# Second biases at eviction or in the residual, router columns beside an identity, expert rows turned amid the tile ahead

## The chip, the cores and the metric

The kernel runs on one core of one Trainium2 chip. The metric is the device time of one execution in microseconds (us). TensorE (PE) multiplies matrices, VectorE (DVE), ScalarE (ACT) and GpSimd (POOL) work elementwise, and SyncE (SP) issues most DMA transfers. Each engine takes its instructions in the order in which the program lists them for it, and waits on semaphores for the others.

## The reference

Two layers of attention and feed-forward parts run over x of shape (16, 256, 256) in float32. The change lies in the last line, the mixture of experts:

```python
h = gelu(x @ fc1_w.T + fc1_b)                      # conditioned part, exact gelu
y = concat([h @ fc2_w.T + fc2_b, h @ We.T + be])   # 192 shared columns, 64 of the sequence's own expert
probs = softmax(y @ w_router.T)                    # 8 experts
gates = the two largest probs, else 0
acc = gelu(y @ Ws1.T + bs1) @ Ws2.T + bs2          # shared expert, tanh gelu
acc = acc + sum over e of gates[e] * (gelu(y @ W1[e].T + b1[e]) @ W2[e].T + b2[e])
x = x + acc / sqrt(1 + 2 / 8)
```

There are 4096 tokens (16 sequences of 256), model width 256, hidden width 1024. The factor 1 / sqrt(1.25) is `OUT_SCALE`.

## The kernel before, in words

`woven(k)` computes everything ahead of the mixture, in an order planned by `weave`, and writes x to memory. It is not touched. `mixture` (from line 1034) then works on tiles of 128 tokens, four to a block, eight blocks. Its instructions are ordered by the framework: each engine's list follows a planned schedule in which ready instructions of a later block may go ahead of an earlier one's. PSUM banks come from two rings of four, `bank0` and `bank1`, chosen by `k.stream`; a ring gives out a bank again when its readers are done.

- `conditioned` (L1340), once per block: eight transposes of x (`transposed`, L99; copies alternate between ACT and DVE, L113), fc1 with exact gelu, the shared and own columns of fc2 into `yT` (features on partitions), router logits with a matmul of 8 columns (L1401), then `route`.
- `route` (L1202): softmax and the two best experts on DVE, with a short exp on ACT. `r.g` takes the gates (L1225), with a ninth column of ones. Small bf16 matmuls count how many tokens went to each expert before. Then y is turned back to tokens on partitions (L1255) and copied into one of three buffers `r_y` (L1257). GpSimd scatters the rows by indirect DMA into `ysort`, sorted by expert (L1259), two scatters per tile of 128 tokens.
- `plan_tiles` (L1267) works out which expert each tile of 256 sorted rows belongs to.
- `shared_block` (L1087): the shared expert on a block. The gates are transposed to `gT` (L1093, L1094). After the eight matmuls of the second layer a ninth, `gT` against `k.b2` (L1108), adds the sum over experts of gate times b2, and bs2 by the column of ones. DVE adds the scaled bank to x (L1111). Four blocks run before the experts, four after.
- `expert_tile` (L1114): 39 at most, 35 of them always, the last four within a branch that isn't taken with these inputs. Per tile: index and b1 are copied to `own_b1`, SP reads expert and row from it, loads `ys` (256 rows), `w1` and `w2`; four transposes turn `ys` to `ysT`; 16 matmuls with gelu (L1140), 16 more, a copy to `o` (L1145), a store to `osort`. Two buffers each. In the built order the transposes of two tiles stand together ahead of the first of them.
- `combine` (L1149): GpSimd gathers a token's two expert rows from `osort`, DVE adds them by their gates to x, SP stores.

Of the kernel before, what the change touches and what calls it, by code (L numbers as in the profile page):

```python
# [19 lines left out]
P = 128  # L20
S = 256
D = 256
# [1011 lines left out]
def mixture(k, out):  # L1034

    nc, tc, a = k.nc, k.tc, k.a
    B, NT = k.B, 2 * k.B
    with ExitStack() as ctx:  # L1040
        k.ps = ctx.enter_context(tc.tile_pool(name="ps", bufs=4, space=bass.MemoryType.PSUM))
        keep = ctx.enter_context(tc.tile_pool(name="moe_keep", bufs=1))

        k.xs = keep.tile([P, NT, D], F32, name="xs")
        for b in range(B):
            nc.sync.dma_start(out=k.xs[:, 2 * b : 2 * b + 2, :], in_=k.xd[b].rearrange("(s p) d -> p s d", p=P))
        k.hp = ctx.enter_context(tc.tile_pool(name="moe_h", bufs=2))
        k.p2 = ctx.enter_context(tc.tile_pool(name="moe_p2", bufs=2))
        k.yT = keep.tile([P, 2, B * S], F32, name="yT")
        k.b1 = keep.tile([P, NE + 1, 8], F32, name="b1")  # L1050
        k.b2 = keep.tile([NE + 1, D], F32, name="b2")
        nc.sync.dma_start(out=k.b1, in_=a["b1"])
        nc.sync.dma_start(out=k.b2, in_=a["b2"])
        r = routing_state(k, keep)
        w1s = keep.tile([P, 2, FF1], F32, name="w1s")
        w2s = keep.tile([P, 8, D], F32, name="w2s")
        nc.sync.dma_start(out=w1s, in_=a["w1"][NE])
        nc.sync.dma_start(out=w2s, in_=a["w2"][NE])
        conditioned(k, keep, r)
        k.stream = 1  # L1060
        plan_tiles(k, keep, r)

        ew = ctx.enter_context(tc.tile_pool(name="moe_w", bufs=2))
        early = 4
        for blk in range(early):
            k.stream = blk % 2
            shared_block(k, r, w1s, w2s, blk)
        for t in range(k.n_tiles - SPARE):
            k.stream = t % 2
            expert_tile(k, ew, r, t)  # L1070

        used = nc.values_load(r.used[0:1, 0:1], min_val=0, max_val=k.n_tiles)
        with tc.If(used > k.n_tiles - SPARE):
            for t in range(k.n_tiles - SPARE, k.n_tiles):
                k.stream = t % 2
                expert_tile(k, ew, r, t)
        for blk in range(early, NT // 4):

            for t in range(4 * (blk - early), 4 * (blk - early) + 4):
                combine(k, r, t, out)  # L1080
            k.stream = blk % 2
            shared_block(k, r, w1s, w2s, blk)
            for t in range(4 * blk, 4 * blk + 4):
                combine(k, r, t, out)


def shared_block(k, r, w1, w2, blk):  # L1087

    nc = k.nc
    gT = k.p2.tile([NE + 1, 512], F32, name="gT", tag="gT")  # L1090
    pt = bank(k)
    for i in range(4):
        nc.tensor.transpose(pt[: NE + 1, i * P : (i + 1) * P], r.g[:, 4 * blk + i, :], k.ident)  # L1093
    nc.vector.tensor_copy(gT, pt[: NE + 1, :])  # L1094
    hT = k.hp.tile([P, 8, 512], F32, name="hT", tag="hT")
    for f in range(8):
        ph = bank(k)
        mm(
            nc,
            ph,  # L1100
            [(w1[:, c, f * P : (f + 1) * P], k.yT[:, c, blk * 512 : (blk + 1) * 512]) for c in range(2)],
        )
        nc.scalar.activation(hT[:, f, :], ph, AF.Gelu_apprx_tanh, bias=k.b1[:, NE, f : f + 1])  # L1103
    for t4 in range(4):
        t = 4 * blk + t4
        po = bank(k)[:, :D]
        pairs = [(hT[:, f, t4 * P : (t4 + 1) * P], w2[:, f, :]) for f in range(8)]
        pairs.append((gT[:, t4 * P : (t4 + 1) * P], k.b2))  # L1108
        mm(nc, po, pairs)
        x = k.xs[:, t, :]  # L1110
        nc.vector.scalar_tensor_tensor(x, po, OUT_SCALE, x, ALU.mult, ALU.add)  # L1111


def expert_tile(k, pool, r, t):  # L1114

    nc, a = k.nc, k.a

# [9 lines left out]
    nc.sync.dma_start(out=ys, in_=k.ysort[bass.ds(row, TT), :].rearrange("(c p) d -> p c d", p=P))  # L1127
    nc.sync.dma_start(out=w1, in_=a["w1"][bass.ds(e, 1)].rearrange("e p c f -> p (e c) f"))
    nc.sync.dma_start(out=w2, in_=a["w2"][bass.ds(e, 1)].rearrange("e p f d -> p (e f) d"))
    ysT = k.p2.tile([P, 2, TT], F32, name="ysT", tag="ysT")  # L1130
    transposed(
        k,
        ysT.rearrange("p c (s t) -> p (c s) t", t=P),
        [ys[:, s, c * P : (c + 1) * P] for c in range(2) for s in range(2)],
    )
    hT = k.p2.tile([P, 8, TT], F32, name="ehT", tag="ehT")
    for f in range(8):
        ph = bank(k)[:, :TT]
        mm(nc, ph, [(w1[:, c, f * P : (f + 1) * P], ysT[:, c, :]) for c in range(2)])
        nc.scalar.activation(hT[:, f, :], ph, AF.Gelu_apprx_tanh, bias=b1[:, f : f + 1])  # L1140
    po = bank(k).rearrange("p (s d) -> p s d", s=2)
    for s in range(2):
        mm(nc, po[:, s, :], [(hT[:, f, s * P : (s + 1) * P], w2[:, f, :]) for f in range(8)])
    o = k.p2.tile([P, 2, D], F32, name="eo", tag="eo")
    nc.vector.tensor_copy(o, po)  # L1145
    nc.sync.dma_start(out=k.osort[t * TT : (t + 1) * TT, :].rearrange("(c p) d -> p c d", p=P), in_=o)


def combine(k, r, t, out):  # L1149
# [19 lines left out]
def routing_state(k, keep):  # L1169
    nc = k.nc  # L1170
    NT = 2 * k.B
    r = Routing()
    r.g = keep.tile([P, NT, NE + 1], F32, name="g_all")
    nc.gpsimd.memset(r.g, 1.0)
    r.hot = keep.tile([P, TOPK, NT, NE], F32, name="hot")
    r.rank = keep.tile([P, NT, NE], F32, name="rank")
    r.gate = keep.tile([P, TOPK, NT], F32, name="gate")
# [21 lines left out]
    return r  # L1199


def route(k, r, pool, logits, t0, n):  # L1202

    nc = k.nc
    B_ = lambda t: t.unsqueeze(2).to_broadcast([P, n, NE])
# [16 lines left out]
    nc.vector.tensor_tensor(gt, gt, eq, ALU.add)  # L1222
    place = pool.tile([P, n, NE], F32, name="r_place", tag="r_place")
    nc.vector.tensor_reduce(place, gt, AX.X, ALU.add)
    nc.vector.scalar_tensor_tensor(r.g[:, t0 : t0 + n, 0:NE], place, TOPK - 0.5, p, ALU.is_lt, ALU.mult)  # L1225
    tmp = pool.tile([P, n, NE], F32, name="r_tmp", tag="r_tmp")
    for i in range(TOPK):
        hot = r.hot[:, i, t0 : t0 + n, :]
# [20 lines left out]
    nc.vector.tensor_copy(posi, pos)  # L1249

    for t in range(n):
        pt = bank(k)[:, :D]
        tok = slice((t0 + t) * P, (t0 + t + 1) * P)
        for c in range(2):
            nc.tensor.transpose(pt[:, c * P : (c + 1) * P], k.yT[:, c, tok], k.ident)  # L1255
        y = pool.tile([P, D], F32, name="r_y", tag="r_y", bufs=3)
        copies(k)(y, pt)  # L1257
        for i in range(TOPK):
            nc.gpsimd.indirect_dma_start(  # L1259
                out=k.ysort[:, :],  # L1260
                out_offset=bass.IndirectOffsetOnAxis(ap=posi[:, i, t : t + 1], axis=0),
                in_=y,
                in_offset=None,
            )

# [74 lines left out]
def conditioned(k, keep, r):  # L1340
# [3 lines left out]
    with ExitStack() as ctx:  # L1344
# [9 lines left out]
        fc1b = load("fc1b", [P, 8], a["fc1b"])  # L1354
        fc2 = load("fc2", [P, 8, P], a["fc2a"])
        fc2b = load("fc2b", [P, 1], a["fc2_b"][0:P].unsqueeze(1))
        wr = load("wr", [P, 2, NE], a["w_router"])
        expb = load("expb", [16, 64], a["L1_cond2_experts_b"])

        bias2 = w.tile([P, B], F32, name="bias2")  # L1360
# [11 lines left out]
        for blk in range(NT // 4):  # L1372
            k.stream = blk % 2
            for b in (2 * blk, 2 * blk + 1):
# [18 lines left out]
            for i in range(2):  # L1393
# [1 line left out]
                py = bank(k)[:, :S]  # L1395
                mm(nc, py, [(own[b % 3][:, f, :], hT[:, f, i * S : (i + 1) * S]) for f in range(8)])
                nc.vector.tensor_scalar(k.yT[:, 1, b * S : (b + 1) * S], py, bias2[:, b : b + 1], None, ALU.add)
# [112 lines left out]
```

## Time and profile before

| | |
|---|---|
| median of 3 runs | 2944.68 us (2943.74 to 2948.99) |
| the profiled execution | 2943.53 us, its span 2941.8 us |
| mean clock granted to TensorE | 0.963 |
| TensorE busy over the span | 2768.7 us, 94% |
| DVE, ACT, POOL busy | 1428.6, 924.0, 842.2 us |
| first transposes of the mixture | 1907.59 us from the start |
| conditioned blocks | routers from 1955.29 us to 2173.97 us |
| first expert transposes | 2301.67 us |
| last four shared blocks | from 2812.74 us |

In a group's name `out<-in` the tiles are named without their numbers; a line can be that of a helper, so L49 stands for every matmul made by `mm`. An f32 matmul appears as two instructions. TensorE's instructions overlap, so differences between starts say more than lengths do. A wait is put down to the releaser that came last.

### The profile page before, as it was taken

Reading aid. Unit: us, or ns where it says so; the run is one execution under the profiler, and the core shown is the slowest. Engines: PE = TensorE matmul, PEld = TensorE weight load, DVE = VectorE, ACT = ScalarE, POOL = GpSimd, SP = SyncE. Lnnn points to the kernel's source line nnn. Section 1 sums busy time; section 2 is a strip of 40 time slices with the busy share of each in tenths; the row PEclk is TensorE's granted clock in tenths of the full one; section 3 lists DMA queues with packets and bytes.
Section 4 is the critical chain, followed back from the end, with each engine's and each line's share of the span. In section 5 each row is a group of like instructions: output and inputs, shape, how many; then the busy total and the mean of one; then the engine's idle time right before and its main releaser. Section 6 shows DMA issues by size and latency. Waiting matters only on the chain. (4 is left out here: it accounts for less than half of the span.)

```text
span 2941.8 us, 42036 instructions
## 1 busy us (share of the span) xinstructions
PE 2768.7 (94%) x15979; PEld 2072.5 (70%) x15979; DVE 1428.6 (49%) x3073; ACT 924.0 (31%) x2416; POOL 842.2 (29%) x1023
## 2 busy tenths in 40 slices
PE   5899999999999999999999989689999999999999
PEld 3666667777777777767777767545566888888865
DVE  6566666676676676675776655413240000000023
ACT  2223333333333333423334333223321222222221
POOL 4333333433344343343343333202220000000034
PEclk7799999999899999999999999889999999999999
DMA  3122122122122132222221222231111355555523
GB/s 107 55 93 73 53 92 84 56 80 74 59 91 69 58 97 69 63 92 69 64 92 35 76 90 74 87 93 51 51 38 67 108 179 179 179 181 179 177 85 95
DMA packets 191230, 265.66 MB, mean 90 GB/s; under 512 B 34217, under 2 KB 161970, under 8 KB 181682
## 3 DMA queue, kind: packets, MB, share of 16 engines
q1 hardware_dynamic: 184882, 246.16, 26.2%
q0 software_dynamic: 6144, 16.79, 1.8%
q8 instruction: 128, 2.10, 0.3%
q14 instruction: 76, 0.62, 0.1%
HBM read 202.34 MB, written 60.56 MB: 89 GB/s over the span
## 5 line engine op out<-in xcount | busy, mean ns | idle before, releaser
L160 ACT ACTIVATE f_prob<-pair,f_stat 128x144 f32<-128x144 f32 x512 | 190.7, 377 | 270.2 <-DVE f_stat L160 258.8
L160 DVE TENSOR_TENSOR pair<-pair,mask 128x256 f32<-128x256 f32 (+1 forms) x384 | 197.8, 516 | 123.1 <-PE pair L160 83.2
L49 PE MATMUL bank<-ysT,w 128*128 128x256 f32 x1120 | 249.3, 381 | 5.7 <-ACT ysT L113 5.7
L160 PE MATMUL single<-e_zT,wq 128*128 128x256 f32 x1024 | 254.1, 392 | 0.0
L1155 POOL DMA_INDIRECT got<-osort,pos_o x64 | 62.3, 973 | 662.8 <-ACT hT L1103 608.5
L49 PE MATMUL bank<-w,ehT 128*128 128x256 f32 x1120 | 247.4, 379 | 0.0
L49 PEld LDWEIGHTS bank<-ysT,w 128*128 128x128 f32 x1120 | 211.3, 190 | 38.0 <-ACT ysT L113 9.9
L49 PEld LDWEIGHTS bank<-w,ehT 128*128 128x128 f32 x1120 | 212.8, 190 | 28.9
L160 PEld LDWEIGHTS single<-e_zT,wq 128*128 128x128 f32 x1024 | 193.4, 196 | 32.9 <-issue 2.7
L1140 ACT ACTIVATE ehT<-bank,own_b 128x256 f32<-128x256 f32 x280 | 132.5, 473 | 241.6 <-PE bank L49 241.6
L160 POOL TENSOR_SCALAR_AFFINE_SELECT b_e<-b_e 128x512 f32<-128x512 f32 x128 | 86.5, 676 | 329.9 <-ACT b_e L160 329.9
L160 PE MATMUL pair<-keys,f_q 32*128 32x144 f32 x2048 | 164.9, 300 | 0.9 <-ACT b_e L160 0.7
L160 PEld LDWEIGHTS pair<-keys,f_q 32*128 32x128 f32 x2048 | 137.2, 190 | 35.9 <-issue 28.6
L160 ACT ACTIVATE b_e<-pair 128x768 f32<-128x768 f32 x128 | 103.6, 810 | 166.4 <-PE pair L160 153.3
L160 PE MATMUL single<-wo,f_oT 128*128 128x256 f32 x512 | 129.8, 386 | 9.5 <-ACT f_oT L160 8.4
L160 POOL TENSOR_TENSOR f_q<-f_t,f_t 128x256 f32<-128x256 f32 x128 | 91.6, 734 | 160.9 <-DVE f_t L160 151.4
L160 PE MATMUL pair<-b_qkT 16*128 16x128 f32 (+1 forms) x1024 | 127.3, 373 | 11.0 <-ACT b_qkT L160 8.0
L1145 DVE COPY eo<-bank 128x512 f32<-128x512 f32 x35 | 24.2, 692 | 230.9 <-PE bank L49 230.9
L160 DVE TENSOR_REDUCE qpad<-pair 128x2 f32<-128x256 f32 (+1 forms) x256 | 131.0, 554 | 4.4
L1259 POOL DMA_INDIRECT ysort<-r_y,r_posi x64 | 62.6, 978 | 241.0 <-DMA ysort<-r_y,r_posi 97.0
L160 DVE TENSOR_TENSOR x<-x,single 128x512 f32<-128x512 f32 (+1 forms) x112 | 68.0, 607 | 128.7 <-PE single L160 128.1
L160 POOL TENSOR_TENSOR keys<-f_t,f_t 128x256 f32<-128x256 f32 x128 | 95.2, 762 | 118.8 <-DVE f_t L160 117.6
(295 smaller groups left out, 5319.7 us busy)
## 6 DMA issues: line engine op xcount, KB each, us to landing
w<-in_w SPq DMA_DIRECT2D x70, 1024.0 KB
ysort<-zero SPq DMA_DIRECT2D x32, 1024.0 KB
wq<-in_w_qk SPq DMA_DIRECT2D x128, 256.0 KB
wv<-in_w_v SPq DMA_DIRECT2D x64, 256.0 KB
wo<-in_w_out SPq DMA_DIRECT2D x64, 256.0 KB
ys<-ysort SPq DMA_DIRECT2D x35, 256.0 KB
osort<-eo SPq DMA_DIRECT2D x35, 256.0 KB
xT<-in_xT SPq DMA_DIRECT2D x16, 256.0 KB
```

The source lines that it names most:

```text
L49: nc.tensor.matmul(out, lhsT, rhs, start=start and i == 0, stop=stop and i == last)
L160: return Op([(self.name, self.cost(fn, outs, aps), lambda: call(*args, **kw))], outs, aps)
L1140: nc.scalar.activation(hT[:, f, :], ph, AF.Gelu_apprx_tanh, bias=b1[:, f : f + 1])
L1145: nc.vector.tensor_copy(o, po)
L1155: nc.gpsimd.indirect_dma_start(out=g, out_offset=None, in_=k.osort[:, :], in_offset=bass.IndirectOffsetOnAxis(ap=r.pos_o[:, i, t : t + 1], ...
L1259: nc.gpsimd.indirect_dma_start(out=k.ysort[:, :], out_offset=bass.IndirectOffsetOnAxis(ap=posi[:, i, t : t + 1], axis=0), in_=y, in_offset ...
```

## The change

The second biases leave TensorE. bs2, times `OUT_SCALE`, is broadcast over the partitions, and GpSimd adds it to a block's x once that block's x has been transposed. Each expert's b2 is loaded with its weights, broadcast, and added when a tile's bank is evicted; so the gates need no transposing and `r.g` is gone.

The router's matrix gets an identity of 128 columns ahead of its 8: one matmul of 136 columns per half of the features gives the half of y turned to tokens, and that half's share of the logits. The two shares lie side by side in a bank; DVE copies one and adds the other to it. y is copied out before routing, into one of five buffers, and `route` gets it as `ys`.

`expert_tile` becomes `expert_rows` (loads and transposes) and `expert_tiles` (the rest), and the rows of tile t + 1 are asked for between the two matmul runs of tile t. In the built order tiles 0 and 1 are still turned together, and each later tile's transposes stand between the runs of the tile ahead. The order on SP keeps a tile's loads of ys, w1 and w2 ahead of the store of o two tiles before; the load of b2 stands behind that store.

```diff
-        k.b2 = keep.tile([NE + 1, D], F32, name="b2")
+        k.bs2 = keep.tile([P, D], F32, name="bs2")
         nc.sync.dma_start(out=k.b1, in_=a["b1"])
-        nc.sync.dma_start(out=k.b2, in_=a["b2"])
+        nc.sync.dma_start(out=k.bs2, in_=a["b2"][NE : NE + 1].to_broadcast([P, D]))
+        nc.vector.tensor_scalar(k.bs2, k.bs2, OUT_SCALE, None, ALU.mult)
...
-        for t in range(k.n_tiles - SPARE):
-            k.stream = t % 2
-            expert_tile(k, ew, r, t)
+        expert_tiles(k, ew, r, range(k.n_tiles - SPARE))
...
@@ def shared_block
-    gT = k.p2.tile([NE + 1, 512], F32, name="gT", tag="gT")
-    pt = bank(k)
-    for i in range(4):
-        nc.tensor.transpose(pt[: NE + 1, i * P : (i + 1) * P], r.g[:, 4 * blk + i, :], k.ident)
-    nc.vector.tensor_copy(gT, pt[: NE + 1, :])
...
-        pairs = [(hT[:, f, t4 * P : (t4 + 1) * P], w2[:, f, :]) for f in range(8)]
-        pairs.append((gT[:, t4 * P : (t4 + 1) * P], k.b2))
-        mm(nc, po, pairs)
+        mm(nc, po, [(hT[:, f, t4 * P : (t4 + 1) * P], w2[:, f, :]) for f in range(8)])
...
-def expert_tile(k, pool, r, t):
+def expert_rows(k, pool, r, t):
+    k.stream = t % 2
...
     nc.sync.dma_start(out=w2, in_=a["w2"][bass.ds(e, 1)].rearrange("e p f d -> p (e f) d"))
+    b2 = k.p2.tile([P, D], F32, name="eb2", tag="eb2")
+    nc.sync.dma_start(out=b2, in_=a["b2"][bass.ds(e, 1)].to_broadcast([P, D]))
     ysT = k.p2.tile([P, 2, TT], F32, name="ysT", tag="ysT")
     transposed(
...
+    return ysT, w1, w2, b1, b2
+
+def expert_tiles(k, pool, r, tiles):
+    nc = k.nc
+    rows = expert_rows(k, pool, r, tiles[0])
+    for t in tiles:
+        ysT, w1, w2, b1, b2 = rows
+        k.stream = t % 2
+        hT = k.p2.tile([P, 8, TT], F32, name="ehT", tag="ehT")
+        for f in range(8):
+            ph = bank(k)[:, :TT]
+            mm(nc, ph, [(w1[:, c, f * P : (f + 1) * P], ysT[:, c, :]) for c in range(2)])
+            nc.scalar.activation(hT[:, f, :], ph, AF.Gelu_apprx_tanh, bias=b1[:, f : f + 1])
+        if t + 1 in tiles:
+            rows = expert_rows(k, pool, r, t + 1)
+            k.stream = t % 2
+        po = bank(k).rearrange("p (s d) -> p s d", s=2)
+        for s in range(2):
+            mm(nc, po[:, s, :], [(hT[:, f, s * P : (s + 1) * P], w2[:, f, :]) for f in range(8)])
+        o = k.p2.tile([P, 2, D], F32, name="eo", tag="eo")
+        nc.vector.tensor_tensor(o, po, b2.unsqueeze(1).to_broadcast([P, 2, D]), ALU.add)
...
@@ def routing_state
-    r.g = keep.tile([P, NT, NE + 1], F32, name="g_all")
-    nc.gpsimd.memset(r.g, 1.0)
...
@@ def route
-    nc.vector.scalar_tensor_tensor(r.g[:, t0 : t0 + n, 0:NE], place, TOPK - 0.5, p, ALU.is_lt, ALU.mult)
...
-        pt = bank(k)[:, :D]
-        tok = slice((t0 + t) * P, (t0 + t + 1) * P)
-        for c in range(2):
-            nc.tensor.transpose(pt[:, c * P : (c + 1) * P], k.yT[:, c, tok], k.ident)
-        y = pool.tile([P, D], F32, name="r_y", tag="r_y", bufs=3)
-        copies(k)(y, pt)
...
-                in_=y,
+                in_=ys[t],
...
@@ def conditioned
-        wr = load("wr", [P, 2, NE], a["w_router"])
+        wr = w.tile([P, 2, P + NE], F32, name="wr")
+        nc.sync.dma_start(out=wr[:, :, P:], in_=a["w_router"])
+        nc.vector.tensor_copy(wr[:, :, 0:P], k.ident.unsqueeze(1).to_broadcast([P, 2, P]))
...
+            x = k.xs[:, 4 * blk : 4 * blk + 4, :]
+            nc.gpsimd.tensor_tensor(x, x, k.bs2.unsqueeze(1).to_broadcast([P, 4, D]), ALU.add)
...
-            pl = bank(k)[:, : 4 * NE].rearrange("p (t e) -> p t e", e=NE)
+            logits = p2.tile([P, 4, NE], F32, name="logits", tag="logits")
+            part = p2.tile([P, 4, NE], F32, name="part", tag="part")
+            ys = []
             for t4 in range(4):
                 tok = slice(blk * 512 + t4 * P, blk * 512 + (t4 + 1) * P)
-                mm(nc, pl[:, t4, :], [(k.yT[:, c, tok], wr[:, c, :]) for c in range(2)])
-            logits = p2.tile([P, 4, NE], F32, name="logits", tag="logits")
-            nc.vector.tensor_copy(logits, pl)
-            route(k, r, p2, logits, 4 * blk, 4)
+                py = bank(k)[:, : 2 * (P + NE)].rearrange("p (c w) -> p c w", c=2)
+                for c in range(2):
+                    mm(nc, py[:, c, :], [(k.yT[:, c, tok], wr[:, c, :])])
+                nc.vector.tensor_copy(part[:, t4, :], py[:, 1, P:])
+                nc.vector.tensor_tensor(logits[:, t4, :], py[:, 0, P:], part[:, t4, :], ALU.add)
+                y = p2.tile([P, 2, P], F32, name="r_y", tag="r_y", bufs=5)
+                copies(k)(y, py[:, :, 0:P])
+                ys.append(y.rearrange("p c d -> p (c d)"))
+            route(k, r, p2, logits, ys, 4 * blk, 4)
```

More of the change, by code (lines that the diff above doesn't have):

```diff
@@ L1067, in mixture @@
             shared_block(k, r, w1s, w2s, blk)
-        for t in range(k.n_tiles - SPARE):
-            k.stream = t % 2
-            expert_tile(k, ew, r, t)
+        expert_tiles(k, ew, r, range(k.n_tiles - SPARE))
         used = nc.values_load(r.used[0:1, 0:1], min_val=0, max_val=k.n_tiles)
         with tc.If(used > k.n_tiles - SPARE):
-            for t in range(k.n_tiles - SPARE, k.n_tiles):
-                k.stream = t % 2
-                expert_tile(k, ew, r, t)
+            expert_tiles(k, ew, r, range(k.n_tiles - SPARE, k.n_tiles))
         for blk in range(early, NT // 4):
@@ L1135, in expert_tile @@
     )
[L1136 to L1146, printed above, removed]
+    return ysT, w1, w2, b1, b2
[18 more added lines that the diff above has]
+        nc.vector.tensor_tensor(o, po, b2.unsqueeze(1).to_broadcast([P, 2, D]), ALU.add)
+        nc.sync.dma_start(out=k.osort[t * TT : (t + 1) * TT, :].rearrange("(c p) d -> p c d", p=P), in_=o)
 def combine(k, r, t, out):
@@ L1199, in routing_state, with route @@
     return r
-def route(k, r, pool, logits, t0, n):
+def route(k, r, pool, logits, ys, t0, n):
     nc = k.nc
```

## The prediction

> **What bounds the kernel now.** I read the page's slices first, then the stretches from 1926 us on, which are the mixture, and there TensorE's own waits. The page says TensorE is busy 94% of the span, but that is a mean over a woven part that this change leaves alone. Three stretches of the mixture, with the busy time of each engine:
>
> ```profile
> core 0: us, PE busy (x) PEld busy (x) DVE busy (x) ACT busy (x) POOL busy (x), PEclk, DMA share, GB/s
> 2048.45:2079.83 31.38, 31.38 (x121) 18.71 (x120) 8.96 (x37) 9.51 (x14) 7.67 (x8) 1.00 0.17 51
> ...
> 2330.73:2359.79 29.06, 28.77 (x137) 25.17 (x136) 2.56 (x7) 8.16 (x17) 0.00 (x0) 1.00 0.54 182
> 2844.51:2875.15 30.64, 30.64 (x105) 18.89 (x105) 9.46 (x21) 5.50 (x8) 15.63 (x16) 1.00 0.34 100
> ```
>
> They are one block of the conditioned stage, two expert tiles, and one shared block without its first transposes. TensorE fills each at clock 1.00 and nobody else is half busy, so here a TensorE instruction removed is time removed, until somebody is late. The waits of TensorE from 1990 to 2302 us are none; from 2302 to 2812 us there is one kind:
>
> ```profile
> PE bank L49 <- ACT ysT L113: 5.7, 18, 0.7
> ```
>
> The timeline of a shared block shows what its bias costs (start, length, line, tile, count):
>
> ```profile
> 2270.49 0.60 PE L1093 MATMUL bank<-ident,g_all 128*9 128x128 f32 x4
> 2270.93 13.90 PE L49 MATMUL bank<-yT,w1s 128*128 128x512 f32 x32
> 2284.67 3.62 PE L49 MATMUL bank<-w2s,hT 128*128 128x256 f32 x16
> 2288.22 0.69 PE L49 MATMUL bank<-b,gT 9*128 9x256 f32 x2
> 2288.84 3.72 PE L49 MATMUL bank<-w2s,hT 128*128 128x256 f32 x16
> 2292.49 0.69 PE L49 MATMUL bank<-b,gT 9*128 9x256 f32 x2
> ```
>
> Lengths overlap, so I work with distances of starts. An f32 matmul is two instructions. 32 of 512 columns take 13.74 us (2270.93 to 2284.67), 0.429 each. A token group with its bias recurs every 4.27 us (2288.22 to 2292.49).
>
> An expert pair (requests are on SP's queue):
>
> ```profile
> 2326.11 0.38 SPq L1127 DMA_DIRECT2D ys<-ysort  x1
> 2330.73 1.04 PE L107 MATMUL bank<-ident,ys 128*128 128x128 f32 x8
> 2331.42 0.58 ACT L113 COPY ysT<-bank 128x512 f32<-128x512 f32 x1 [6.92 <-PE bank L107]
> 2332.06 7.17 PE L49 MATMUL bank<-ysT,w 128*128 128x256 f32 x32 [0.29 <-ACT ysT L113]
> ```
>
> Within a pair the runs of 32 follow each other at 6.90 us (2316.92, 2323.82, 2330.73), so 0.2157 a matmul instruction. The turning plus its wait is 1.33 us (2330.73 to 2332.06), of which eight transposes are 0.92.
>
> The router of a block:
>
> ```profile
> 1985.70 1.18 PE L49 MATMUL bank<-wr,yT 128*128 128x8 f32 x10
> 1986.73 0.74 PE L107 MATMUL bank<-ident,xs 128*128 128x128 f32 x5
> 1987.31 0.73 PE L49 MATMUL bank<-wr,yT 128*128 128x8 f32 x6
> 1987.90 0.52 PE L107 MATMUL bank<-ident,xs 128*128 128x128 f32 x3
> 1988.26 6.37 PE L49 MATMUL bank<-g_xT,fc 128*128 128x512 f32 x14
> ...
> 1994.67 1.07 PE L1255 MATMUL bank<-ident,yT 128*128 128x128 f32 x8
> ```
>
> Ten matmul instructions of 8 columns take 1.03 us, 0.103 each; a transpose 0.115. The turning of y holds TensorE 0.91 us (1994.67 to the next start, 1995.58).
>
> **What the Trainium skill says.** "TensorE: Matmul & The Clock Gate", LDWEIGHTS: the load's time goes with the columns of the weights, not with the rows contracted. The trace agrees: gT's 9-row loads have a median of 182 ns, 128-row ones 190. A bias of 9 rows is priced like a full matmul. "FP8 and Floating Point Precision", TensorE Precision Notes: true FP32 takes four passes; 0.429 and 0.2157 us for 512 and 256 columns, two instructions to a matmul, fit that. "SBUF — State Buffer", Who interferes with whom: a VectorE instruction with two SBUF inputs contends with a GpSimd one that reads SBUF. In this kernel's router stage GpSimd computes nothing, so no trace of before shows it. "DMA: Bandwidth & Descriptors", Specifications: pieces under 512 B are below line rate; it bears on wr's loading.
>
> **1. Shared blocks (8).** Gone are four transposes of g_all (0.44 us), one copy on DVE, and four bias matmuls. From 2239.32 to 2270.49 a block is 31.17 us. What stays is 13.74 + 64 x 0.2157 = 13.81, together 27.55. Gain 3.62 us, which is more than the 8 bias instructions at 0.2157 (1.73) plus 0.44: the rest is the switch to 9 rows and back. 8 x 3.62 = **29.0 us**. In the last four blocks GpSimd's gathers must keep up: 16 of them 1.25 us apart are 20 us, in a block of 27.5, and two per token group (2.5 us) against a group of 3.45. Before, GpSimd still waited 6.5 us in each of those blocks, so TensorE stays the bound and the end (evict, two adds, store) moves with it. With that cover gone the price would be at most a few us at the very end.
>
> **2. Expert tiles (35).** By the built streams, TensorE turns tiles 0 and 1 together, then tile t+1 between the two matmul runs of tile t. Per pair before: 29.06. After, a tile is 6.91 + 0.46 + 6.90, and the ysT copies (0.58 on ACT, 0.69 on DVE) lie under the 6.9 us second run. Before, 2301.67 to about 2810.95 is 509.3. After: 1.33 + 0.1 first fill + 35 x 13.81 + 33 x 0.46 = 500.0. Gain **9.3 us**. Bounds: no gain if four transposes inside a tile cost an exposed 0.27 more than at its edge; not above 9.4, since only the waits go.
> What moves with it: the eviction adds b2 instead of copying; an add from PSUM of the same 128x512 is 0.69 us in the woven part, the copy 0.69, so nothing. The new 128 KB load of b2 stands on SP after the store of o, whose buffers it also waits for; about 0.4 us of SP plus its register setup, against an SP gap of over 5 us before the next request. It is needed a tile later. DMA share goes from 0.54 by a twentieth. On DVE the index copy that SP waits for now stands, for every second tile, behind the ysT copy, so requests slip about 1.4 us. ys is due at the end of the first run of the next tile: 6.9 x 2 less about 3.7, plus 0.5, is 10.5 us after its request. In the profile above the pair's second ys was asked for at 2326.11 and used from about 2331.2 with no wait, so it lands within 5.1 us.
>
> **3. Router (8 blocks).** Removed: eight transposes, 0.91. Widened: 16 instructions from 8 to 136 columns. From 0.429 and 0.2157 the slope is 0.000833 us a column, so 136 columns are 0.116 against 0.103: +0.2. Blocks 0 and 7 gain 0.7 each. Between blocks 1 to 6 and their successors the old order split the router's matmuls around xs transposes; the built stream has all 16, then all 8. The fourth transpose then ends at 1.86 + 0.46 = 2.32 us after the router's start, the ACT copy begins 0.24 later and takes 0.58, and the next matmuls start at 3.19 instead of 2.56. Against this +0.63 stand 0.91 and about 0.2 of an old wait for the second copy: gain 0.48 each.
> VectorE has six more small operations a block, and evicts y before it routes (0.42 twice on DVE, twice on ACT); r_p comes about 0.4 us later by that. GpSimd's addition of bs2, 128x1024, is 1.9 us by its f_prob multiplication of that shape in the woven part, and falls about 3 us after the router's start, just when routing uses two SBUF inputs; if it blocks them, sel comes another 1.1 us later, at about +8.9 to +9.7, and TensorE wants it at +9.3. I take 0.2 us of wait per block, bounds 0 and 0.6. Sum 1.4 + 6 x (0.48 - 0.2) = **3.1 us**, from -1 to 5.
> Behind DVE's y copy stands the second xT copy, for which TensorE waits. That copy needs one of five y buffers, freed when six scatters of the block before are done. Scatters follow each other like this:
>
> ```profile
> 2074.39 0.96 POOL L1259 DMA_INDIRECT ysort<-r_y,r_posi  x1 [1.71 <-DMA ysort<-r_y,r_posi]
> 2077.55 0.96 POOL L1259 DMA_INDIRECT ysort<-r_y,r_posi  x1 [2.20 <-DVE yT L1397]
> ```
>
> They start 12.1 us after the router (2048.45 to 2060.55); the sixth is done by +29.1. The copy falls at 30.7 + 2.6 = 33.3. Slack 4 us, or 2 to 3 if routing is late; 1 to 2 for block 0, whose scatters shared the queues with weights.
>
> **4. Start of the mixture.** TensorE waits for expb until 1923.48. Ahead of it in the queue bs2 now moves 128 KB instead of 9, 0.4 us at the about 330 GB/s of those 20 us, and wr 256 pieces of 32 B instead of 128 of 64. The new DVE copies (wr 0.4, bs2 0.4) lie in DVE's idle 19.96 us there, and GpSimd drops a memset off the path. Loss **0.6 us**, bounds 0 and 3.
>
> **Sum.** 29.0 + 9.3 + 3.1 - 0.6 = 40.8. The profiled execution took 2943.5 (span 2941.8), so 2902.7 (span 2901.0). The median of the runs is 1.2 above it: **2903.9 us**.
>
> **Rivals.**
> - The router gives its gain back: y buffers or GpSimd's addition make TensorE wait 1 to 3 us in seven blocks. For it: the thin slack of block 0. Against it: 4 us elsewhere. 2911 to 2925. Chance 0.12.
> - The expert order doesn't pay: transposes amid a tile cost 0.27 us more than at its edge. Against it: 2330.73 follows the run before without a gap. 2913. Chance 0.08.
> - Slower: ys is late for its new, earlier place. TensorE would stop in 34 tiles in front of the transposes. Every us that ys lands beyond 10.5 after its request costs 34; from 11.7 it eats all 40.8, and at 13 the time is 2989. Against it: the 5.1 us bound, at a DMA share of 0.54. Chance 0.03.
> - A little more than forecast, where bank or copy waits that I left in vanish at the start or the branch: 2890 to 2896. Chance 0.05.
> - Nothing moves, within 0.2% (6 us, about what a measurement of this kernel can tell from no change): it needs two of the losses together. Chance 0.01.
> The forecast has 0.71, its own range 2897 to 2911. The range to 2894 and 2917 takes in most of the first two rivals and part of the fourth. Faster 0.95, same 0.01, slower 0.04.
>
> **What would show it.** Shared blocks 27.5 us apart with no line of g_all or gT. Expert tiles 14.27 us apart, with TensorE's wait for ysT once. Routers 30.7 us apart, their 16 instructions in 1.9, and a wait of 0.4 for the g_xT copy. Wrong would be: TensorE waiting for ys from DMA; DVE's r_y copies waiting for DMA with g_xT behind them; TensorE waiting for r_sel over 0.5 us; a clock under 1.00 after 1960 us.

## The result, and the profile after

The changed kernel takes 2901.68 us in the median of five runs (2893.57 to 2905.76), the kernel before 2944.68 us beside it. The ratio is 0.9853, with a 95% interval of 0.9836 to 0.9870. The forecast was 2903.9 us. The profiled execution took 2904.1 us, its span 2902.4 us, 39.4 us below the span before.

The five runs span 12 us, so that the median lies 2.2 us from the forecast is partly luck; the parts show more. Where the 39.4 us lie, as distances between starts of TensorE's instructions in the two profiles:

| stretch | before | after | difference | forecast |
|---|---|---|---|---|
| start of the span to the first router | 1955.29 | 1955.85 | +0.6 | +0.6 |
| eight routers (0.7, 6 x 0.08, 0.8; worked out below) | | | -1.9 | -3.1 |
| shared blocks, each | 31.17 | 27.55 | 8 x -3.62 = -29.0 | -29.0 |
| first expert transposes to the late shared blocks | 511.07 | 501.47 | -9.6 | -9.3 |
| after the last shared block: last additions and stores | | | +0.5 | 0 |

The expert row has the pause at the branch in it, for which TensorE waits 2.0 us in the changed kernel and 1.6 in the kernel before; without the pause the gain there is 10.0 us.

The same kinds of stretches as shown for before, each with the busy time of every engine: one conditioned block, two expert tiles, one shared block:

```profile
2048.18:2079.48 31.30, 30.83 (x113) 18.19 (x112) 11.32 (x43) 9.42 (x14) 10.06 (x9) 1.00 0.17 51
2287.11:2315.62 28.51, 28.51 (x134) 25.13 (x135) 1.81 (x7) 8.17 (x17) 0.00 (x0) 1.00 0.42 143
2814.92:2842.47 27.55, 27.55 (x98) 18.24 (x96) 9.28 (x20) 5.50 (x8) 16.84 (x18) 1.00 0.44 127
```

TensorE still fills the expert and shared stretches. The first row is the only one in which it no longer does: 31.30 us long, 30.83 busy. The missing 0.47 is in the list of its waits from 1956 to 2302 us (total, times, longest). Before, this list was empty here.

```profile
PE bank L49 <- ACT g_xT L113: 2.7, 6, 0.5
PE bank L49 <- ACT ysT L113: 0.2, 1, 0.2
```

The second line stands for the experts: one wait of 0.2 where there were 18. In TensorE's timeline an expert tile's turning stands between two full runs, without a gap, every 14.25 us:

```profile
2457.80 7.07 PE L49 MATMUL bank<-ysT,w 128*128 128x256 f32 x32
2464.71 0.60 PE L107 MATMUL bank<-ident,ys 128*128 128x128 f32 x4
2465.14 7.07 PE L49 MATMUL bank<-w,ehT 128*128 128x256 f32 x32
```

A shared block is two lines in place of ten, and the next block follows at 2258.28:

```profile
2230.74 13.90 PE L49 MATMUL bank<-yT,w1s 128*128 128x512 f32 x32
2244.47 13.98 PE L49 MATMUL bank<-w2s,hT 128*128 128x256 f32 x64
```

The router of a block:

```profile
2048.18 2.02 PE L49 MATMUL bank<-wr,yT 128*128 128x136 f32 x16
2050.04 1.04 PE L107 MATMUL bank<-ident,xs 128*128 128x128 f32 x8
2051.55 6.28 PE L49 MATMUL bank<-g_xT,fc 128*128 128x512 f32 x14 [0.47 <-ACT g_xT L113]
2057.66 0.17 PE L49 MATMUL bank<-r_sel,earlier 128*128 128x8 bf16 x1
...
2057.90 3.25 PE L49 MATMUL bank<-g_xT,fc 128*128 128x512 f32 x7
```

fc1 starts 3.37 us after the router (2.57 before) and goes on after the counting matmuls (L49, r_sel and seen) at +9.72 (+9.88 before). Most of the router's story lies between these two numbers, and most of the experiments are about them.

### The profile page after: what moved, and what is told of

Its sections match the earlier page's. It is cut to its first block, busy times and chain, and to the rows that moved or that the text cites. A ratio compares the mean times of both kernels' runs of the same rounds, so it can differ in the third digit from the quotient of the medians.

```text
span 2902.4 us, 41871 instructions
## 1 busy us (share of the span) xinstructions
PE 2728.9 (94%) x15819; PEld 2056.7 (71%) x15819; DVE 1437.1 (50%) x3115; ACT 925.0 (32%) x2416; POOL 862.8 (30%) x1030
## 5 line engine op out<-in xcount | busy, mean ns | idle before, releaser
L49 PE MATMUL bank<-ysT,w 128*128 128x256 f32 x1120 | 247.5, 379 | 0.2 <-ACT ysT L113 0.2
L49 PE MATMUL bank<-w,ehT 128*128 128x256 f32 x1120 | 247.5, 379 | 0.0
L49 PEld LDWEIGHTS bank<-ysT,w 128*128 128x128 f32 x1120 | 212.7, 190 | 29.4 <-ACT ysT L113 0.5
L49 PEld LDWEIGHTS bank<-w,ehT 128*128 128x128 f32 x1120 | 210.2, 190 | 27.2
L1152 DVE TENSOR_TENSOR eo<-bank,eb 128x512 f32<-128x512 f32 x35 | 24.2, 692 | 234.4 <-PE bank L49 234.4
L160 PE MATMUL pair<-b_qS,b_qkT 17*128 17x256 f32 (+1 forms) x1024 | 121.7, 357 | 6.2 <-DVE qpad L160 2.8
```

What stands on the lines that cost most here:

```text
L49: nc.tensor.matmul(out, lhsT, rhs, start=start and i == 0, stop=stop and i == last)
L160: return Op([(self.name, self.cost(fn, outs, aps), lambda: call(*args, **kw))], outs, aps)
L1152: nc.vector.tensor_tensor(o, po, b2.unsqueeze(1).to_broadcast([P, 2, D]), ALU.add)
```

## Experiments

The woven part ahead of the mixture varies by over ten us from execution to execution: the first router starts between 1944.9 and 1959.2 us in profiles of kernels whose woven part is the same, and before's own medians beside these experiments lay between 2936.0 and 2943.3. So small effects are read in distances inside the mixture, which repeat to 0.1 us, but for the pause at the branch (0.9 to 2.0 us). For the eight conditioned blocks I use the distance from the first router to the second shared block's first matmul, less one shared block, and in the kernels with g_all less 0.43 us for its first transposes. It is 221.7 us before and 219.8 after: the router's 1.9.

### Biases alone, on the kernel before

```diff
-        k.b2 = keep.tile([NE + 1, D], F32, name="b2")
+        k.bs2 = keep.tile([P, D], F32, name="bs2")
...
-    gT = k.p2.tile([NE + 1, 512], F32, name="gT", tag="gT")
...
-        pairs.append((gT[:, t4 * P : (t4 + 1) * P], k.b2))
...
-    nc.vector.tensor_copy(o, po)
+    nc.vector.tensor_tensor(o, po, b2.unsqueeze(1).to_broadcast([P, 2, D]), ALU.add)
...
+            nc.gpsimd.tensor_tensor(x, x, k.bs2.unsqueeze(1).to_broadcast([P, 4, D]), ALU.add)
```

> The kernel before with the biases alone: bs2 added by GpSimd in the conditioned stage, b2 at the expert tiles' eviction, no g_all, no gT, no bias matmul. My theory: the shared blocks give what they gave in the whole change, 8 x 3.62 = 29.0 us, each 27.55 apart; the larger load of bs2 costs at most 0.4 at the start; the addition at the eviction costs nothing. 2944.7 - 28.6 = 2916. In the old router VectorE's r_p stands 0.2 us later than the addition's start too, so the addition delays r_sel by up to 1.8 us; if TensorE waits for that, blocks 1 to 6 of the conditioned stage are 31.4 to 33 apart instead of 31.38, and the time is 2916 to 2926. Rival: the gain belonged to the three parts together; this part alone gives less than 26.

Measured: 2917.05 us against 2943.27 of before beside it, ratio 0.9922 (0.9896 to 0.9948). Shared blocks are 27.55 apart, expert tiles as before. But the conditioned blocks grew by 5.0 us (221.7 to 226.7), blocks 3 to 6 from 31.38 to 31.96 each, blocks 1 and 2 more (33.22 and 32.15). VectorE's r_p takes 1.83 us there instead of 0.18 and ends with GpSimd's addition (2045.92 and 2045.87). So the 29.0 us are the biases' own, the rival falls, and the addition has a price, 5 us in this company; whether all of the 5 us is the addition's, the experiments with the old router and with the additions moved take up.

### Expert order alone, on the kernel before

```diff
-        for t in range(k.n_tiles - SPARE):
-            k.stream = t % 2
-            expert_tile(k, ew, r, t)
+        expert_tiles(k, ew, r, range(k.n_tiles - SPARE))
```

(with `expert_rows` and `expert_tiles` of the change, without b2)

> The kernel before with the expert order alone: tile t+1's rows are turned between the two matmul runs of tile t, b2 stays in the shared blocks. My theory: tiles 14.25 to 14.27 apart instead of 14.53 a tile, one wait for ysT instead of 18, so 9.3 to 9.6 us less: 2935.1. Rival: part of the 9.6 came from the eviction or from b2's load; then less than 9 here and the rest in the biases alone. The conditioned stage and the shared blocks stay as before (31.38 and 31.17 apart).

Measured: 2934.0 us against 2943.27, ratio 0.9976 (0.9964 to 0.9988). From the first expert transposes to the first late matmul 501.61 us instead of 511.50, so 9.9 us less; conditioned and shared blocks to 0.01 as before. The order's gain is its own. The whole change has 9.6 and not 9.9 because its pause at the branch is 0.4 longer, so b2's load and addition at the eviction cost nothing that shows.

### The changed kernel with the old router

```diff
-        wr = w.tile([P, 2, P + NE], F32, name="wr")
+        wr = load("wr", [P, 2, NE], a["w_router"])
...
+        for c in range(2):
+            nc.tensor.transpose(pt[:, c * P : (c + 1) * P], k.yT[:, c, tok], k.ident)
+        y = pool.tile([P, D], F32, name="r_y", tag="r_y", bufs=3)
+        copies(k)(y, pt)
```

> The changed kernel with the old router: wr without an identity, y turned by eight transposes after routing; GpSimd's addition of bs2 stays in the conditioned stage. Theory A, that the router's small gain is what the widened matmuls give less a later copy on ScalarE, and that the addition costs TensorE nothing in either order: blocks 1 to 6 at 31.38, block 0 and 7 each 0.7 longer than in the changed kernel, 2901.7 + 1.9 = 2903.6. Theory B, that the addition delays routing and TensorE waits for r_sel in the old order: blocks over 31.6, 2905 or more, and the new router is worth more than its 1.9 us in this company.

Measured: 2909.38 us against 2943.27, ratio 0.9892 (0.9855 to 0.9929). The eight blocks take 226.1 us, 6.3 more than in the changed kernel. Theory B holds, A falls. GpSimd's and VectorE's timelines show the place (this kernel's router starts at 2049.59):

```profile
2052.41 2.35 POOL L1390 TENSOR_TENSOR xs<-xs,bs 128x1024 f32<-128x1024 f32 x1 [1.05 <-PE bank L107]
```

```profile
2052.97 1.83 DVE L1214 TENSOR_TENSOR r_p<-logits,r_st 128x32 f32<-128x32 f32 x1
2058.25 0.19 DVE L1239 TENSOR_TENSOR r_sel<-hot 128x32 bf16<-128x32 f32 x1
```

r_p, two inputs in SBUF, ends at 2054.80 with the addition (2054.76); before it took 0.18. r_sel is ready at 2058.44, and TensorE's counting matmuls start at 2058.49, +8.90 instead of +8.77. They then stretch over 0.66 us instead of 0.20, as they come in step with VectorE's small additions to `seen`. The turning of y stands behind them, and fc1 goes on at +10.46 instead of +9.88: the 0.58 us.

### The changed kernel, additions behind the last routing

```diff
@@ def conditioned
-            nc.gpsimd.tensor_tensor(x, x, k.bs2.unsqueeze(1).to_broadcast([P, 4, D]), ALU.add)
@@ def mixture, after plan_tiles
+        nc.vector.tensor_scalar(one, r.gate[:, 0, NT - 1 : NT], -1.0, None, ALU.is_gt)
+        nc.vector.tensor_scalar(k.bs2, k.bs2, one, None, ALU.mult)
         for blk in range(early):
             k.stream = blk % 2
             shared_block(k, r, w1s, w2s, blk)
+            for q in (blk, blk + early):
+                x = k.xs[:, 4 * q : 4 * q + 4, :]
+                nc.gpsimd.tensor_tensor(x, x, k.bs2.unsqueeze(1).to_broadcast([P, 4, D]), ALU.add)
```

(`one` is always 1.0; it makes the addition depend on the last block's gates)

> The changed kernel with GpSimd's eight additions of bs2 moved behind the last block's routing (among the first four shared blocks). My theory: VectorE's r_p takes 0.18 us again instead of 1.83, r_sel is there 1.65 us earlier, but TensorE was hardly waiting for it: 0 to 0.2 us a block, blocks 31.1 to 31.3 apart, 2900.5 to 2901.7. The wait for the g_xT copy on ScalarE, 0.4 to 0.5 us in each of blocks 0 to 6, stays. Rival: the addition is what took the router's gain; then blocks 0.3 us shorter or more, 2899.5 or less.

Measured: 2901.72 us, ratio 0.9867 (0.9835 to 0.9899). r_p takes 0.18 us, r_sel's instruction starts at +8.04 us after the router instead of +8.82, blocks are 31.26 apart instead of 31.30, and the eight take 219.5 instead of 219.8:

```profile
2054.84 0.18 DVE L1220 TENSOR_TENSOR r_p<-logits,r_st 128x32 f32<-128x32 f32 x1
```

The theory holds: in the new router the addition costs 0.3 us in all. Of the 1.65 us that r_p loses only 0.78 reach r_sel, since the exp behind r_p then waits for ScalarE's load of its table.

With before, the biases alone and the changed kernel this closes a square, in us for the eight blocks:

| | without the addition | with it |
|---|---|---|
| old router | 221.7 | 226.1 and 226.7 |
| new router | 219.5 | 219.8 |

The field at 221.7 is the kernel before, which also has its gate transposes and bias matmuls, in the shared blocks, and VectorE's write of g_all (0.19 us) in the routing; the two at 226 differ in the expert order. The long r_p in both is what ties the 4.4 to 5 us to the addition.

### The changed kernel, addition made twice

```diff
-        nc.vector.tensor_scalar(k.bs2, k.bs2, OUT_SCALE, None, ALU.mult)
+        nc.vector.tensor_scalar(k.bs2, k.bs2, 0.5 * OUT_SCALE, None, ALU.mult)
...
-            nc.gpsimd.tensor_tensor(x, x, k.bs2.unsqueeze(1).to_broadcast([P, 4, D]), ALU.add)
+            for _ in range(2):
+                nc.gpsimd.tensor_tensor(x, x, k.bs2.unsqueeze(1).to_broadcast([P, 4, D]), ALU.add)
```

> The changed kernel with GpSimd's addition made in two instructions of the same size, half of bs2 each: the suspected cost doubled. Theory A, that VectorE's instruction with two inputs in SBUF is held until GpSimd's has ended: r_p takes about 4.2 us, r_sel comes 2.3 us later (about 11.1 us after the router's start, where TensorE wants it at 9.4), TensorE waits 1.5 to 2 us for it in each of seven blocks, 2912 to 2916. Rival: r_p's length had another cause; it stays at 1.8 and the time at 2901.7.

Measured: 2913.29 us, ratio 0.9899 (0.9862 to 0.9936); blocks 1 to 6 are 32.80 apart instead of 31.30, 9.0 us in all. Theory A holds, in another form: not one instruction of VectorE is held for 4.2 us, two are held, each until one addition ends. GpSimd's timeline, then VectorE's:

```profile
2051.73 4.76 POOL L1388 TENSOR_TENSOR xs<-xs,bs 128x1024 f32<-128x1024 f32 x2 [1.57 <-PE bank L107]
```

```profile
2052.29 1.84 DVE L1214 TENSOR_TENSOR r_p<-logits,r_st 128x32 f32<-128x32 f32 x1
2054.42 0.19 DVE L1216 TENSOR_REDUCE r_st<-r_p 128x4 f32<-128x32 f32 x1 [0.30 <-ACT r_p L1215]
2054.85 1.69 DVE L1218 TENSOR_TENSOR r_p<-r_p,r_st 128x32 f32<-128x32 f32 x1
```

The reduction between them, with one input, takes its usual 0.19 us while the second addition runs. That agrees with what "SBUF — State Buffer", Who interferes with whom, states in the Trainium skill: VectorE's two-input form meets GpSimd's reads, its one-input form does not.

### The kernel before, bias matmuls of 128 rows

```diff
-        k.b2 = keep.tile([NE + 1, D], F32, name="b2")
+        k.b2 = keep.tile([P, D], F32, name="b2")
+        nc.gpsimd.memset(k.b2, 0.0)
+        k.gTs = [keep.tile([P, 512], F32, name=f"gT{i}") for i in range(2)]
+        for g in k.gTs:
+            nc.gpsimd.memset(g, 0.0)
...
-    gT = k.p2.tile([NE + 1, 512], F32, name="gT", tag="gT")
+    gT = k.gTs[blk % 2]
...
-    nc.vector.tensor_copy(gT, pt[: NE + 1, :])
+    nc.vector.tensor_copy(gT[: NE + 1, :], pt[: NE + 1, :])
```

> The kernel before with gT and b2 filled with zeros to 128 rows, so that the four bias matmuls of a shared block have 128 rows, like their neighbours, instead of 9; the sum is the same. My theory: of the 0.82 us that a bias takes in its token group (4.27 less 16 x 0.2157 = 3.45), 0.43 are its two instructions and 0.39 the change to 9 rows and back; so each of 32 biases costs 0.39 less, shared blocks are 29.6 apart instead of 31.17, and the time is 2944.7 - 12.5 = 2932. Rival: the 0.39 is a wait for gT or for the end of the accumulation; then nothing changes, 2944.7.

Measured: 2931.73 us against 2943.27, ratio 0.9965 (0.9954 to 0.9977). Shared blocks are 29.71 apart instead of 31.17. TensorE's timeline:

```profile
2224.74 3.62 PE L49 MATMUL bank<-w2s,hT 128*128 128x256 f32 x16
2228.19 0.59 PE L49 MATMUL bank<-b,gT 128*128 128x256 f32 x2
2228.62 3.62 PE L49 MATMUL bank<-w2s,hT 128*128 128x256 f32 x16
```

A bias takes 0.43 us (2228.19 to 2228.62) and a group 3.88 instead of 4.27. A bias with 119 rows of zeros is 0.39 us cheaper than one of 9 rows, so that share of the old cost belongs to the 9 rows amid 128. Half of it, 0.20, lies in the run of 16 beside the bias, whose rows did not change (3.65 us before, from 2288.84 to 2292.49, 3.45 here). A wait for gT does not explain it, as gT comes from the same copy. That a stream of 9-row matmuls alone would cost nothing extra was not tried.

### The changed kernel, four buffers for y

```diff
-                y = p2.tile([P, 2, P], F32, name="r_y", tag="r_y", bufs=5)
+                y = p2.tile([P, 2, P], F32, name="r_y", tag="r_y", bufs=4)
```

> The changed kernel with four buffers for y instead of five. My working gave five a slack of 4 us; with four, VectorE's last y copy has to wait for all eight scatters of the block before, the last of which starts 0.5 us after the router's start and takes about 1 us on GpSimd and some 2 us to land. Theory: VectorE's copy waits about 0.5 to 1.5 us, the second g_xT copy behind it comes later, but TensorE needs that only for its second fc1 instruction pair: blocks 31.3 to 32.5 apart, 2902 to 2910. Rival: no wait, because the scatters have read their rows earlier; 2901.7.

Measured: 2908.93 us, ratio 0.9885 (0.9848 to 0.9921), 7.4 us more in the conditioned blocks. VectorE's waits there:

```profile
DVE r_y L1413 <- DMA ysort<-r_y,r_posi: 9.8, 6, 3.1
```

and TensorE's behind them:

```profile
PE bank L49 <- DVE g_xT L113: 4.3, 5, 1.9
PE bank L49 <- ACT g_xT L113: 3.1, 6, 0.8
```

This is the rival of the prediction in which y buffers make TensorE wait, and it comes true with one buffer fewer. With five the copy waits for a scatter two places earlier, some 5 us (scatters start 2.6 to 3.2 us apart), and in block 3 with four it waited 1.4 us: a slack of about 4 us with five, as forecast. Blocks 1 and 2, at 32.6 and 35.4, cost more than the theory's 32.5; the copy waited up to 3.1 us there.

### The changed kernel, ys asked for last

```diff
-    nc.sync.dma_start(out=ys, in_=k.ysort[bass.ds(row, TT), :].rearrange("(c p) d -> p c d", p=P))
     nc.sync.dma_start(out=w1, in_=a["w1"][bass.ds(e, 1)].rearrange("e p c f -> p (e c) f"))
     nc.sync.dma_start(out=w2, in_=a["w2"][bass.ds(e, 1)].rearrange("e p f d -> p (e f) d"))
+    nc.sync.dma_start(out=ys, in_=k.ysort[bass.ds(row, TT), :].rearrange("(c p) d -> p c d", p=P))
```

> The changed kernel with the load of ys issued behind w1 and w2 and, in the built order, behind the store of the tile before's result. In the changed kernel ys is used 11.95 us after its request, with no wait; here the request comes about 6.5 us before its use. Theory, that it lands within 5.1 us: no wait or a few tenths, tiles 14.25 apart, 2901.7 to 2904. Rival, that it lands only after the weights asked for ahead of it, 7 us or more after its request: TensorE waits 0.5 us or more in 33 tiles, 2918 or more.

Measured: 2912.12 us, ratio 0.9901 (0.9869 to 0.9934). From the first expert transposes to the late blocks 510.3 us instead of 501.5: 8.8 us, 0.27 per tile. What the trace says on the tile ys between 2400 and 2700 us:

```profile
DMA to landing us min/median/max: 5.3/5.5/6.8
```

The request at 2448.89 is used at 2454.39, 5.5 us later, just as it lands. Both of my cases missed: it lands behind no queue of weights, but a little later than the 5.1 us that I had taken as its bound. In the changed kernel the request at 2481.26 is used at 2493.21, 11.95 us later, with no wait. So there are over 5 us of slack, and the rival that ends slower than before was far away. Another 1.7 us of this run are the first late shared block, whose first 32 matmuls took 15.51 us after the pause at the branch, against 13.81. Their granted clock was 0.89 on the mean: within a us of TensorE's restart it fell to 0.50, and it was back at 1.00 some 3.4 us later. Two other experiments have the same 1.7 (the addition made twice, and the next but one); five profiles with the same pause of 2.0 us don't, and I don't know why.

### The changed kernel, the next block's x turned ahead of the router

```diff
+            xT = xT_next
...
+            if blk + 1 < NT // 4:
+                xT_next = turn(blk + 1)
             logits = p2.tile([P, 4, NE], F32, name="logits", tag="logits")
```

(`turn` holds the transposes with their copies, and GpSimd's addition; block 0 is turned ahead of the loop)

> The changed kernel with the next block's xs transposes put ahead of the router's matmuls instead of behind them. Theory: the g_xT copies lie under the router, fc1 starts 1.9 us after the router instead of 3.4 us, with 0.92 of transposes ahead: 0.55 to 0.6 us less in each of seven blocks, no wait for g_xT, 2897.7. VectorE's r_p must then not be held by GpSimd's addition, since TensorE wants r_sel at 7.9 us after the router's start instead of 9.4; the addition starts earlier too, with the transposes. Rival: r_sel stays at 8.8 us after the router's start, TensorE waits 0.9 us for it, and nothing is gained: 2901 to 2904.

Measured: 2898.09 us, ratio 0.9861 (0.9833 to 0.9890), not to be told from the changed kernel by its time. The wait for the g_xT copy is gone and a block in the steady part is 30.61 apart, 0.69 less. That is 4.1 us in the six distances which hold a turning. Against it stand two things. A block's turning used to fill TensorE's wait for expb at the start, and now costs 0.9. And r_sel is late in three blocks, which lengthens them by 0.2, 0.4 and 1.8; TensorE's waits in this stage:

```profile
PE bank L49 <- DVE r_sel L1239: 1.8, 2, 1.6
```

From the first fc2 to the second shared block it is 260.2 us instead of 261.1. Of the 4 us of the theory 0.9 are left: a mixture of theory and rival. The late r_sel is GpSimd's addition again: in the block that lost 1.8 us VectorE's r_p took 3.00 us and ended with the addition (2147.35 and 2147.29); where r_p took only 0.5, TensorE did not wait.

### The changed kernel, expb's product and the shared weights later

```diff
-        nc.sync.dma_start(out=w1s, in_=a["w1"][NE])
-        nc.sync.dma_start(out=w2s, in_=a["w2"][NE])
+        k.shared = (w1s, w2s)
...
-        pb = bank(k)
-        mm(nc, pb[64:128, :B], [(expb, k.onehot[0:16, 2, :])])
-        nc.vector.tensor_copy(bias2[64:128, :], pb[64:128, :B])
...
+            if blk == 1:
+                for t, n in zip(k.shared, ("w1", "w2")):
+                    nc.sync.dma_start(out=t, in_=a[n][NE])
...
+            if blk == 0:
+                pb = bank(k)
+                mm(nc, pb[64:128, :B], [(expb, k.onehot[0:16, 2, :])])
+                nc.vector.tensor_copy(bias2[64:128, :], pb[64:128, :B])
```

> The changed kernel with the product of expb (the experts' second bias) made behind the first block's fc2 instead of ahead of its first matmuls, and the loads of w1s and w2s (2 MB) asked for in the second block instead of ahead of the conditioned stage. In the changed kernel TensorE turned the first xs at 1907.7 us and then waited 14.9 us for expb, with fc asked for since 1896. Theory: fc1 starts at about 1910 instead of 1926.8, and nothing else is late for its new time (own is needed about 22 us later, at 1932, and 6 us of transfers stand less ahead of it): 2901.7 - 16 = 2886. Rivals: own or the first xs come late and give half of it back (2893); or TensorE's clock, 0.50 until 1929 in the changed kernel, stays low longer from an earlier start (2888 to 2890).

Measured: 2886.14 us, ratio 0.9826 (0.9803 to 0.9850). The largest wait of TensorE in the mixture, 14.9 us for expb, is gone. TensorE's timeline:

```profile
1902.86 1.95 PE L107 MATMUL bank<-ident,xs 128*128 128x128 f32 x8 [9.22 <-DMA xs<-xd]
...
1905.36 14.64 PE L49 MATMUL bank<-g_xT,fc 128*128 128x512 f32 x32
```

From the last woven matmul (9.22 us ahead of the xs transposes) to the first fc2 it is 26.2 us instead of 46.0. Of these 19.8 us 1.9 go to the first two blocks, where a turning again stands uncovered and expb's product has moved in (0.4), and 1.7 to the slower clock at the first late block; own came in time. That leaves 16 us, as the theory had it, but partly by luck: fc1's start came 19 us earlier and not 16.8, since the first xs, too, came 2.4 us sooner, and 3.6 that the theory did not have were lost again. The two moves were not tried apart.

### All three moves

The diffs of the last two, and of the additions behind the last routing, together.

> The changed kernel with three moves together: expb's product behind the first fc2 and w1s, w2s asked for in the second block; the next block's xs transposes ahead of the router; GpSimd's additions behind the last routing. Theory: the first gives 16 us, the second 4, the third lets r_sel be there at 7.2 us after the router's start, ahead of the 7.9 where TensorE wants it: 2901.7 - 20 = 2881.5. Rival: r_sel is still later than 7.9 and TensorE waits for it, 2884 to 2886.

Measured: 2882.65 us, ratio 0.9803 (0.9779 to 0.9828): the fastest of all, 19 us below the changed kernel; in the profiled executions, from the last woven matmul to the end, it is 23. Blocks are 30.61 apart, the last 29.73, with no wait for r_sel or, but for one of 0.2, for g_xT. From the first fc2 to the second shared block it is 258.3 us, 1.9 less than with the turning alone, although 0.4 for expb's product are now in it. So in this order the addition, which cost 0.3 in the changed kernel, costs about 2.3.

## Why the prediction was right, point by point

The profile moved by 39.4 us where 40.8 were forecast. That is three sizes right or nearly so, and one wrong in its terms: 1.2 us less from the router and 0.5 more at the end, against 0.3 more from the expert tiles.

**1. Shared blocks: right.** 27.55 us each, to the hundredth, no line of g_all or gT, 29.0 in all; the biases alone give them. "The rest is the switch to 9 rows and back" is borne out by the padded matmuls. The late blocks stayed with TensorE.

**2. Expert tiles: right, 0.3 us small.** 9.6 instead of 9.3, or 10.0 without the longer pause at the branch; the order alone gives it. The bound "not above 9.4, since only the waits go" was wrong: the turning of a pair with its wait took 1.33 us, of which the wait was 0.29, and two turnings amid tiles take 0.87. So 0.17 us a pair went beyond the wait. Four transposes inside a tile take 0.43 to 0.44 us of TensorE (2464.71 to 2465.14), no more than at its edge. ys is asked for 11.95 us ahead of its use, not 10.5; the landing bound of 5.1 was a little low (5.3 to 6.8 in the experiment), with no effect.

**3. Router: right in direction, mis-sized: 1.9 us instead of 3.1.** Blocks 0 and 7 gave 0.68 and 0.77 (forecast 0.7 each). In blocks 1 to 6 the forecast was 0.28 each, and 0.08 came. ScalarE's timeline at the place, and then the terms of the sum:

```profile
2050.63 0.37 ACT L1413 COPY r_y<-bank 128x256 f32<-128x256 f32 x1 [0.97 <-PE bank L107]
2050.90 0.59 ACT L113 COPY g_xT<-bank 128x512 f32<-128x512 f32 x1
```

- "the next matmuls start at 3.19" was 3.37, that is +0.80 instead of +0.63. The transposes were on time (router matmuls 1.86, as forecast). But ScalarE's second copy of y stood right ahead of its g_xT copy, which so began 0.86 us after the transposes' start (2050.04) instead of the 0.70 that I had reckoned. I had counted the copies of y as work ahead of routing on VectorE, and not as work ahead of g_xT on ScalarE.
- "About 0.2 of an old wait for the second copy": fc1's first 14 instructions took 6.20 us before and 6.11 after, against 14 x 0.429 = 6.01. Only 0.1 of it went.
- "0.2 us of wait per block" for r_sel: 0.04, by the experiment with the additions moved. The mechanism was right (r_p 1.83 us instead of 0.18), but most of the delay found slack: of 0.78 us at r_sel, 0.04 reached TensorE. The addition itself was sized too small: it takes 2.34 us and not the 1.9 of the f_prob multiplication.
- Another 0.08 per block lies in the fc1 run behind the counting matmuls: 18 instructions are 7.97 us long where they follow the counting directly, as in the new router, and 7.89 where y's turning stands between, as before and in both kernels with the old router and the addition. The cause stays open.

What I missed is that these terms aren't a sum. fc1's later start is what made room for the late r_sel: TensorE comes to the counting matmuls at +9.48 instead of +8.77, and r_sel is ready at +9.0. The same addition costs 5.0 us on the old router (4.4 in the kernel with the new expert order) and 0.3 on the new. Counted part by part, the router is worth 2.2 us without the addition (221.7 to 219.5) and 6.3 with it (226.1 to 219.8). The 1.9 us of the table are the 2.2 less the 0.3.

**4. Start: right, if anything smaller.** +0.5 us from the last woven matmul to the first fc2 (45.5 to 46.0). In the three kernels with the old load of b2 that distance is 45.5 to 45.7, with a wait for expb of 13.8 to 14.1; in the seven that load the wide bs2 and leave the rest of the start as it is, 45.7 to 46.3, with 14.3 to 14.9. So the loss is there, 0.3 us on the mean, at the limit of what these profiles tell. Two of the seven have the old wr (45.7 and 46.3): a price of wr's small pieces doesn't show.

**The rivals.** The y buffers hold with five and not with four; late ys costs 0.27 per tile only when asked for 6.5 us later than it is; transposes amid a tile cost nothing extra. GpSimd's addition was the one nearest to coming true: without the new router it would have taken 5 of the 29 us.

## What to carry to other kernels

A wait that an added instruction causes is worth what its consumer's slack leaves of it: take the distance between "ready" and "wanted" for each order of the work, since removing a wait upstream brings the consumer forward and can turn the next dependency into the wait. When a copy moves ahead on an engine, list what stands behind it on both engines that share the copies. And a part that TensorE doesn't need yet, such as a small bias product whose load is late in a long queue, holds up work that is ready if it stands ahead of it: here moving that product and the shared weights' loads gave 16 us, more than the router and the expert order together.

## What the runs showed that I had not expected

- A two-input instruction of VectorE on 128x32 elements took 1.83 us instead of 0.18, ending within 0.05 us of GpSimd's addition, and two in a row did so when there were two additions.
- GpSimd's addition took 2.34 us, and 2.36 where nothing of the routing ran beside it; the f_prob multiplication of the same 128x1024 took 1.90. Both have a broadcast operand, along different axes; which of axis and operation makes the difference was not tried.
- A 9-row f32 matmul amid 128-row ones cost 0.39 us more than one padded to 128 rows; padding alone made the kernel before 1.46 us per shared block faster.
- After the 2.0 us pause at the branch the clock granted to TensorE fell to 0.50 for some 3.4 us in three of eight profiles, and stayed at 1.00 in five. After the shorter pauses of the other five profiles (0.9 to 1.6 us) it did not fall.
